# A graph-attention kernel on one core: one quad's rows loaded singly by SyncE, and a new order at the end

## Chip, core, metric

The kernel runs on one core of a Trainium2 chip. The metric is the device time of one execution in microseconds (us); of several runs the median is given.

## The reference

200,000 edges lead from `src` to `dst` among 12,500 nodes; `dst` is sorted. The node features are normalised, and a graph attention layer with four heads of 32 values is added to the input:

```
h = relu(layernorm(x));  hn = h @ W_node.T;  e = edge_attr @ W_edge.T
att = leaky_relu(sum([hn[src], hn[dst], e] * a), 0.2)          # one value per edge and head
m = max(segment_max(att, dst), 0);  ex = exp(att - m[dst])
denom = segment_sum(ex, dst) + (E - deg) * exp(-m)
out = x + segment_sum(ex / denom[dst] * hn[src], dst)
```

## The kernel before

Edges are cut into 392 groups of 511 (512 places, the first one for what is carried over from the group before); a group is four chunks of 128 edges (`J = 4`), and four groups are a quad (`QG = 4`). There are 98 quads, counted from 0. First a stage turns all nodes into rows of a table in HBM, `table`, with 137 numbers (548 bytes) a row. Then each quad goes through these steps:

- **Gather.** `gather` (L171 on) lets POOL (GpSimd) issue one indirect DMA per chunk: 128 rows of `table`, one for each partition, picked by `srci`. They land in `ga_all`, which has eight places of one quad each (`QUADS = 8`, place `q % 8`). Sixteen such DMAs are one quad. They are asked for two quads ahead of the logits (`fetch(q + 2)` in `open_logits`) and run when the place is free; a semaphore of the place, `arrived`, counts them. For quad 97 the last, half empty group has two fewer.
- **Logits.** `all_logits` (L1395 on) multiplies edge features `ea` and marks `at` (L658, made by DVE from the targets `db`) on PE, L688 and L691. `ea` is loaded by SyncE (SP) two quads ahead, `db` one quad ahead. From quad 10 on `db` holds bytes and fills a quarter of each of the two places in `db_all`, a tile of 16 KB a partition.
- **Sources.** `add_sources` (L720 on) has ScalarE (ACT) wait for the quad's gathers and copy their source terms to `U` (L735).
- **Softmax.** `softmax(s)` (L771 on) works on two to four quads at once (a "super"): scans on DVE, an exponential on ACT (L877), transposes on PE.
- **Sums.** `sums(q)` (L1061 on) weighs the gathered rows (L1048, L1089), marks targets (`hot`, L1031, L1091) and multiplies on PE (L1122), window by window: `for i in range(m)` goes over the four groups. When a quad's sums are done, its place in `ga_all` is free.
- **Division.** `divide_ranges` (L1315 on) for quads below 75, `divide` (L1360 on) after that, turn sums into results; SyncE stores them.

SyncE has one queue in program order. Loads and stores are put on lists (`due`) and issued by `issue` (L598) at fixed points of these steps. Some take their address from SBUF: `windows` (L584) reads register values, one per window, with `values_load_multi_w_load_instructions`. Quads 0 to 35 have one window, 36 to 74 two, later ones four.

The last quads go through `finale` (L1552 on), where the order of the generators `older` (sums of quads 95 and 96), `turned_stage` and `turned_last` (the last two softmaxes), and the divisions is written out by hand. There POOL weighs some rows too (L1048 on POOL), and one division runs on POOL (`divide_by_gpsimd`). `copied_out` (L995 on) makes `den`, the exponential that a division starts from; the first step of a division is L1371. `const_ps` is one PSUM bank for constants and small operands, such as `share_ps`.

Of the kernel before, what the change touches and what calls it, by code (L numbers as in the profile page):

```python
# [9 lines left out]
F32 = mybir.dt.float32  # L10
BF16 = mybir.dt.bfloat16
I32 = mybir.dt.int32
U8 = mybir.dt.uint8
AF = mybir.ActivationFunctionType
OP = mybir.AluOpType
AX = mybir.AxisListType

P = 128
H, HD = 4, 32
# [9 lines left out]
J = 4  # L29
GE = J * P  # L30
NE = GE - 1
WIDE, NARROW = 112, 80
QG = 4
# [6 lines left out]
QUADS = 8  # L40
# [6 lines left out]
SQUARE = 32  # L47
TWO = 2
HELD = 3
SETS = max(NODE_T, QG * J)  # L50
PAD = 1 << 20

# [17 lines left out]
def kernel(  # L70
# [95 lines left out]
    ga_all = consts.tile([P, QUADS, QG, J, ROW], F32, name="ga")  # L166
    GA, GATHERED = {}, set()
    arrived = [tc.alloc_semaphore(f"rows{k}") for k in range(QUADS)]
    landings = {}

    def gather(q, rows, width, lo, hi):  # L171

        g0, m = quads[q]
        ga = GA[q] = ga_all[:, q % QUADS]
        chunks = lambda i: -(-min(E - (g0 + i) * NE + 1, GE) // P)
        for i in range(lo, hi):
            if chunks(i) < J:
                nc.vector.memset(ga[:, i, chunks(i):, :], 0.0)
        order = [(i, j) for i in range(lo, hi) for j in range(chunks(i))]
        for i, j in order:  # L180
            came = nc.gpsimd.indirect_dma_start(  # L181
                out=ga[:, i, j, 0:width], out_offset=None, in_=rows,
                in_offset=bass.IndirectOffsetOnAxis(ap=srci[:, g0 + i, j:j + 1], axis=0))
            if q >= QUADS:
                came.then_inc(arrived[q % len(arrived)], 16)
                tc.no_tile_sem_insts.add(came.ins.name)
                tc.add_to_no_dep_group(f"rows{q}", came.ins)
                landings[q] = landings.get(q, 0) + 16
# [27 lines left out]
    with tc.manual_schedule():  # L216
# [165 lines left out]
        def fetch_targets(q):  # L382
            g0, m = quads[q]
            n = P if class_of(q)[1] == WIDE else NARROW
            db, rows = db_all[:, q % 2], dst.rearrange("(g e) -> g e", e=GE)
            if q >= OFFSETS:
                db = db.rearrange("p g e -> p (g e)")[:, 0:QG * GE // 4].bitcast(U8)
                db, rows = db.rearrange("p (g e) -> p g e", e=GE), offset
            DB[q] = db
            return [(db[:n, lo:lo + k, :],  # L390
                     rows[g0 + lo:g0 + lo + k].unsqueeze(0).to_broadcast([n, k, GE]))
                    for lo, k in blocks(m, QG if q >= OFFSETS else PLACES_BY)]
# [150 lines left out]
    with tc.tile_pool(name="work", bufs=2) as work, \  # L543
# [13 lines left out]
        kept = WIDE + W + QG * H + 1  # L557
        assert kept + GE // per + 1 <= 512
        kept_ps = const_ps[:, kept:kept + GE // per + 1]
        nc.vector.tensor_copy(lane_ps, lane)  # L560
        nc.vector.tensor_copy(node_ps, node_at)
        nc.vector.tensor_copy(part_ps, part)
# [72 lines left out]
        def fetch_rows(s):  # L635
            g0, m = groups(s)
            dr = DR[s] = turned.tile([SBG * H, NE + 2], I32, name="dr", bufs=2)
            if finer(s) > 1:
# [4 lines left out]
            nc.sync.dma_start(dr[0:H * m, :],  # L643
                              dst_rows[g0:g0 + m, :].unsqueeze(0).to_broadcast([H, m, NE + 2]))

        def open_logits(q):
            if q == supers[of_quad[q]][0]:
                fetch_rows(of_quad[q])
            if q + 2 < nq:
                fetch(q + 2)  # L650
            AT[q] = work.tile([P, QG, GE], BF16, name="at")
# [68 lines left out]
        def add_sources(q):  # L720

            s = of_quad[q]
            g0, m = quads[q]
            s0, sm = groups(s)
            keep_logits(q)
            if s not in U:
                U[s] = turned.tile([P, J, SBG * H], F32, name="U", bufs=2)
            f = finer(s)
            u = U[s][:, 0:J // f, 0:sm * H * f].rearrange("p c (h w) -> p w c h", h=H)[
                :, (g0 - s0) * f:(g0 - s0 + m) * f]  # L730
            if q >= QUADS:
                nc.scalar.wait_ge(arrived[q % len(arrived)],
                                  sum(landings[a] for a in range(QUADS, q + 1)
                                      if a % len(arrived) == q % len(arrived)))
            taken = nc.scalar.copy(u, GA[q][:, :m].rearrange("p g (f c) r -> p (g f) c r", f=f)[  # L735
                :, :, :, R_SRC:R_SRC + H])
            if q >= QUADS:
                tc.declare_no_dep(taken.ins, group=f"rows{q}",
                                  reason="a semaphore counts the gathers of this quad")
                tc.declare_fence(taken.ins, group=f"rows{q}")  # L740
            for kept in (EA, DB, PW, AT):
                del kept[q]
# [10 lines left out]
        def keeps(s):  # L753

            f = finer(s)
            R = groups(s)[1] * H * f
            n = (NE if f == 1 else GE // f) + 1
            dr = DR.pop(s)
            earlier = dr[:R, 0:n]
            if 0 < s < len(supers) - 1:  # L760
                before_ps = ps.tile([P, GE], F32, name="t_ps")
                nc.scalar.copy(before_ps[:R, 0:n], earlier)
                earlier = before_ps[:R, 0:n]
            elif s:
                nc.scalar.copy(kept_ps[:R, 0:n], earlier)
                earlier = kept_ps[:R, 0:n]
            kp = KP[s] = turned.tile([SBG * H, GE + 1], F32, name="kp")
            nc.vector.tensor_tensor(kp[:R, 1:n + 1], dr[:R, 1:n + 1], earlier,
                                    op=OP.is_equal)
# [134 lines left out]
        def complete(window=True, all_due=False):  # L904

            state["step"] += 1
            division = None
            if divisions and "hold" not in state and (
                    all_due or divisions[0][-1] is None or divisions[0][-1] + 2 <= state["step"]):
                division = divisions.pop(0)  # L910
            if begun and window:
                complete_window(*begun.pop())
            if division:
                divide(*division)
# [74 lines left out]
        def due_division():  # L989

            if not divisions:
                copied_out()
            return divisions.pop(0)

        def copied_out():  # L995

            if "to copy" not in state:
                return
            q, i, pt, acc = state.pop("to copy")
            span = class_of(q)[1]  # L1000
            nc.scalar.copy(pt[:1 + span, i, :], acc)

            parts = (2,) if first_fold - 2 <= q < first_fold else ()
            if i + 1 in parts or i == windows_in[q][1] - 1:
                lo = max([at for at in parts if at <= i], default=0)
                den = work.tile([P, QG, H], F32, name="den", bufs=4)
                nc.scalar.activation(den[:1 + span, lo:i + 1, :],
                                     pt[:1 + span, lo:i + 1, R_SRC:R_SRC + H], AF.Exp, scale=-1.0)
                divisions.append((q, pt, den, lo, i + 1, None))
# [51 lines left out]
        def sums(q):  # L1061
# [36 lines left out]
            for i in range(m):  # L1098
# [31 lines left out]
                if not later and i == (2 if k > 1 else 1):  # L1130
                    entered()
                    if k == 1:
                        settled()
                complete(new)
                if k == 1:
                    begun.append((q, i, ga, hot, pt, acc, fc))
                if i == 2 and QUADS <= q < first_fold - 5 and of_quad[q + 1] == s:
# [414 lines left out]
        def finale(s, held_sums):  # L1552

            def step(*of):
                for one in of:
                    next(one, None)

            state["hold"] = True
            turned_stage, last = softmax(s), nq - 1
            last_hot, last_lg = marked(last), last_logits(last)  # L1560
            older = chain(sums(last - 2), sums(last - 1))
            step(turned_stage, last_lg, last_lg, turned_stage)
            together(held_sums)
            step(last_lg, last_lg, turned_stage)
            complete()
            copied_out()
            step(turned_stage, turned_stage)
            together(turned_stage)
            select(s + 1)
            turned_last = softmax(s + 1)  # L1570
            step(older)
            added = divide(*due_division(), whole=False)
            keeps(s + 1)
            step(older)
            added()
            together(check_steps)
            step(older)
            together(last_hot)
            step(older)
            divide(*due_division(), whole=False)()  # L1580
            step(turned_last, turned_last, turned_last, turned_last)
            beside_rows(last - 1)
            RESTED.add(last - 1)
            step(older, turned_last, older, older, turned_last, older)
            divide_by_gpsimd(*due_division())
            together(turned_last)
            topped()
            redo = nc.values_load(flag[0:1, 0:1], min_val=0, max_val=1)
            together(older)
            return redo  # L1590
# [282 lines left out]
```

## Time and profile before

| what | value |
|---|---|
| median of 3 runs | 1997.35 us (1996.39 to 2000.05) |
| profiled execution | 1993.67 us |
| its span from first to last instruction | 1991.8 us |
| busy: POOL, DVE, PE, ACT | 75%, 60%, 57%, 16% of the span |
| mean granted TensorE clock | 0.734 |
| table gathers on POOL | 1494, 946 ns each |

An engine's busy share leaves out register, semaphore and DMA-issuing instructions, so SyncE has none there; what it issues and what it waits for has views of its own, in which it is named SPq. A wait is put down to what ended it. "issue" means that nothing in the profile was waited for.

### The profile page before, as it was taken

To read this page: it belongs to the slowest core of one execution; us is meant where nothing else is said; L and a number is where in the kernel's file an instruction comes from. 1 tells how busy PE (TensorE), PEld (TensorE's weight loads), DVE (VectorE), ACT (ScalarE), POOL (GpSimd) and SP (SyncE) were. 2 spreads that over 40 slices of the span, in tenths; PEclk is the share of its full clock that TensorE was granted. 3 is DMA by queue.
4 is the path that set the end of the run, shared out by engine and by line. 5 is a ranking of instruction groups with operands and counts; after the bars stand their busy time and mean duration, and the time that the engine had idled before them with its cause. 6 is when DMAs were issued, how large, how long until landed. Compare 5 with 4: busy or idle time off the path is not lost. (4 is left out here: it accounts for less than half of the span.)

```text
span 1991.8 us, 18871 instructions
## 1 busy us (share of the span) xinstructions
PE 1140.5 (57%) x5116; PEld 780.2 (39%) x5116; DVE 1193.3 (60%) x2615; ACT 318.3 (16%) x1077; POOL 1491.3 (75%) x1585
## 2 busy tenths in 40 slices
PE   6566676556464655554646555546465555455565
PEld 5444454334243433342434333334343333233344
DVE  8676786456374554564746546647465474367676
ACT  6564111001011010010110100101000011122122
POOL 7777777777777777777777777777777777777774
PEclk9788788676676776767767767677777666777778
DMA  7754754434344444344444444444444444444442
GB/s 254 209 141 98 175 132 111 105 93 110 97 108 104 119 98 114 96 108 112 119 101 113 106 110 108 108 114 115 104 107 105 105 120 98 112 109 116 99 106 51
DMA packets 167748, 229.57 MB, mean 115 GB/s; under 512 B 60827, under 2 KB 100669, under 8 KB 167638
## 3 DMA queue, kind: packets, MB, share of 16 engines
q0 software_dynamic: 50112, 109.61, 24.7%
q1 hardware_dynamic: 115824, 116.14, 20.5%
q10 hardware_dynamic: 1702, 2.59, 0.4%
q8 instruction: 41, 0.67, 0.1%
q14 instruction: 69, 0.57, 0.1%
HBM read 210.74 MB, written 17.43 MB: 115 GB/s over the span
## 5 line engine op out<-in xcount | busy, mean ns | idle before, releaser
L181 POOL DMA_INDIRECT ga<-table,srci x1494 | 1413.7, 946 | 456.0 <-issue 407.9
L1122 PE MATMUL acc<-ga,hot 128*113 128x137 f32 (+1 forms) x2928 | 546.2, 346 | 81.5 <-DVE hot L1031 53.6
L1122 PEld LDWEIGHTS acc<-ga,hot 128*113 128x113 f32 (+1 forms) x2928 | 486.5, 216 | 182.2 <-issue 100.4
L956 DVE SCALAR_TENSOR_TENSOR pt<-pt,spare,acc 1x133 f32<-1x133 f32 x113 | 38.3, 339 | 523.5 <-ACT den_of L950 522.1
L691 PE MATMUL lg<-at,pw 112*96 112x512 bf16 (+2 forms) x392 | 157.2, 438 | 278.7 <-DVE at L658 265.8
L688 PE MATMUL lg<-ea,by_pair 128*96 128x512 f32 (+1 forms) x392 | 229.6, 671 | 7.1 <-ACT tg L701 7.1
L658 DVE TENSOR_TENSOR at<-const_ps,db 112x1024 bf16<-112x1024 f32 (+1 forms) x176 | 212.8, 1210 | 3.3 <-DMA db<-offset 3.3
L1089 DVE TENSOR_TENSOR ga<-ga,ex_ps 128x1056 f32<-128x1056 f32 x147 | 182.2, 1239 | 0.0
L792 PE MATMUL t_ps<-ident,U 128*64 128x128 f32 (+2 forms) x210 | 47.2, 397 | 208.9 <-ACT U L735 208.9
L735 ACT COPY U<-ga 128x64 f32<-128x64 f32 x98 | 29.0, 297 | 806.5 <-DMA ga<-table,srci 806.5
L1091 DVE TENSOR_TENSOR hot<-const_ps,slot 128x896 f32<-128x896 f32 (+1 forms) x147 | 144.1, 980 | 0.0
L792 PEld LDWEIGHTS t_ps<-ident,U 128*64 128x64 f32 (+2 forms) x210 | 37.1, 201 | 234.9 <-ACT U L735 231.6
L887 PE MATMUL ex_ps<-ident,stack 128*128 128x128 f32 x105 | 28.6, 424 | 170.2 <-DVE stack L879 157.0
L975 PEld LDWEIGHTS acc<-pt,spare 1*2 1x2 f32 x226 | 14.1, 86 | 209.0 <-issue 200.8
L691 PEld LDWEIGHTS <-pw 112*96 112x96 bf16 (+2 forms) x392 | 54.4, 139 | 102.2 <-issue 99.1
L887 PEld LDWEIGHTS ex_ps<-ident,stack 128*128 128x128 f32 x105 | 18.5, 215 | 184.3 <-ACT stack L877 184.3
L1048 DVE TENSOR_TENSOR ga<-ga,ex_ps 128x528 f32<-128x528 f32 x92 | 63.6, 693 | 38.6 <-ACT xs L893 38.5
L181 POOL DMA_INDIRECT ga<-in_x_dram,srci x72 | 68.3, 948 | 23.2 <-issue 19.2
L701 ACT COPY tg<-lg 96x512 f32<-96x512 f32 (+1 forms) x51 | 29.5, 578 | 293.8 <-PE lg L691 284.4
L920 PE MATMUL acc<-ga,hot 128*81 128x137 f32 x176 | 43.2, 334 | 52.7 <-ACT ga L928 50.8
L717 PE MATMUL t_ps<-tg,of_head 96*64 96x512 f32 (+3 forms) x96 | 72.5, 848 | 0.0
L717 PEld LDWEIGHTS t_ps<-tg,of_head 96*64 96x64 f32 (+3 forms) x96 | 12.0, 174 | 154.1 <-issue 150.9
(209 smaller groups left out, 1318.6 us busy)
## 6 DMA issues: line engine op xcount, KB each, us to landing
ea<-in_edge_t_dram SPq DMA_DIRECT2D x196, 256.0 KB
ga<-table,srci POOLq DMA_INDIRECT x1494
db<-offset SPq DMA_DIRECT2D x53, 256.0 KB
db<-in_dst_dram SPq DMA_DIRECT2D x20, 320.0 KB
db<-offset SPq DMA_DIRECT2D x35, 160.0 KB
table<-row SPq DMA_DIRECT2D x9, 616.5 KB
xt<-in_x_dram SPq DMA_DIRECT2D x9, 576.0 KB
inputs<-in_x_dram SPq DMA_DIRECT2D x92, 56.0 KB
```

The source lines that it names most:

```text
L181: came = nc.gpsimd.indirect_dma_start(out=ga[:, i, j, 0:width], out_offset=None, in_=rows, in_offset=bass.IndirectOffsetOnAxis(ap=srci[:, ...
L658: nc.vector.tensor_tensor(AT[q][:span, i:i + n, :].rearrange("p g e -> p (g e)"), part_ps[:span].to_broadcast([span, n * GE]), DB[q][:span ...
L688: nc.tensor.matmul(lg, by_pair[:, begin:begin + n], ea[:, i // 2, :], start=half == 0 and i == 0, stop=False, skip_group_check=True)
L691: nc.tensor.matmul(lg, PW[q][:span, begin:begin + n], at[:span, i, :], start=False, stop=full and i == quads[q][1] - 1, skip_group_check=True)
L717: nc.tensor.matmul(TP[s][:groups(s)[1] * H], of_head[supers[s][1], p][:n], tg[:n], start=p == 0, stop=False, skip_group_check=True)
L792: nc.tensor.matmul(t_ps[:R, j * P:(j + 1) * P], u[:, j, :R], ident, start=False, stop=j == C - 1, skip_group_check=True)
L887: nc.tensor.transpose(turned_ps[:, j, :], stack[:, j * P:(j + 1) * P], ident)
L920: nc.tensor.matmul(acc, hot[:, i, 0, 0:acc.shape[0]], ga[:, i, 0, :], start=False, stop=stop)
L1048: engine.tensor_tensor(val, val, weight.unsqueeze(3).to_broadcast([P, J, H, HW]), op=OP.mult)
L1089: nc.vector.tensor_tensor(val, val, weight.unsqueeze(3).to_broadcast([P, TWO * J, H, HW]), op=OP.mult)
L1091: nc.vector.tensor_tensor(hot[:, i:i + TWO, :, 1:1 + span].rearrange("p g j c -> p (g j) c"), lane_ps[:, 0:span].unsqueeze(1).to_broadcast ...
L1122: nc.tensor.matmul(acc, hot[:, i, j, 0:1 + span], ga[:, i, j, :], start=new and j == J - 1 and not second, stop=k > 1 and i % k == k - 1 a ...
```

## The change

Quad 84 (the 85th) is no longer gathered by POOL. Its 2048 rows are loaded by SyncE, one DMA a row, into a part of `db_all` that is free from quad 10 on; for that, the two places of `db` lie next to each other at its start. The loads are spread over the sums of quads 11 to 74: after each window, `single_rows` issues eight of them; every second time it first reads sixteen addresses into registers. The addresses of a chunk (128 source numbers) are loaded into one partition sixteen windows ahead (`fetch_places`) and scaled to bytes by DVE (`scale_places`). ScalarE waits for two semaphores, each counting half of the rows, before it copies the quad's source terms.

At the end, `den` of quad 95's first division lies in PSUM, and the steps of `finale` have another order.

```diff
+SINGLE, SINGLES_FROM, AT_A_STEP = 84, 11, 8
...
     def gather(q, rows, width, lo, hi):
+        if q == SINGLE:
+            return
...
             if q >= OFFSETS:
-                db = db.rearrange("p g e -> p (g e)")[:, 0:QG * GE // 4].bitcast(U8)
+                at = q % 2 * QG * GE // 4
+                db = db_all.rearrange("p k g e -> p (k g e)")[:, at:at + QG * GE // 4].bitcast(U8)
...
+        GA[SINGLE] = own[:, QG * GE // 2:QG * GE // 2 + n_own].bitcast(F32).rearrange(
+            "p (g j r) -> p g j r", g=QG, j=J)
...
+        def fetch_places(n):
+            if n >= QG * J:
+                return
+            g, j = quads[SINGLE][0] + n // J, n % J
+            at = ((g // 2 * J + j) * 2 + g % 2) * P
+            nc.sync.dma_start(places[n % 2], src[at:at + P].unsqueeze(0))
+        def scale_places(n):
+            if n < QG * J:
+                nc.vector.tensor_scalar(places[n % 2], places[n % 2], float(4 * ROW), None,
+                                        op0=OP.mult)
+        def single_rows():
+            if not single["step"]:
+                fetch_places(0)
+                scale_places(0)
+            n, at = divmod(single["step"], steps)
+            if n >= QG * J:
+                return
+            single["step"] += 1
+            if not at:
+                fetch_places(n + 1)
+            if at == steps // 2:
+                scale_places(n + 1)
+            lo = at * AT_A_STEP
+            if at % 2 == 0:
+                single["values"] = nc.values_load_multi_w_load_instructions(
+                    places[n % 2][:, lo:lo + 2 * AT_A_STEP], engines=[mybir.EngineType.SP], ...)[1]
+            for p in range(lo, lo + AT_A_STEP):
+                came = nc.sync.dma_start(
+                    as_bytes(GA[SINGLE][p:p + 1, n // J, n % J, :]),
+                    rows_at(table, single["values"][p - at // 2 * 2 * AT_A_STEP], 4 * ROW, 1))
+                came.then_inc(single_came[2 * n // (QG * J)], 16)
...
             if q == SINGLE:
+                for came in single_came:
+                    nc.scalar.wait_ge(came, single["landings"] // 2)
...
-                den = work.tile([P, QG, H], F32, name="den", bufs=4)
+                den = den_ps if q == first_fold - 2 and not lo else work.tile(
+                    [P, QG, H], F32, name="den", bufs=4)
...
                 complete(new)
+                if q >= SINGLES_FROM:
+                    single_rows()
...
             turned_last = softmax(s + 1)
-            step(older)
-            added = divide(*due_division(), whole=False)
-            keeps(s + 1)
-            step(older)
-            added()
+            step(older, older)
+            divide(*due_division(), whole=False)()
             together(check_steps)
             step(older)
+            keeps(s + 1)
             together(last_hot)
             step(older)
             divide(*due_division(), whole=False)()
-            step(turned_last, turned_last, turned_last, turned_last)
             beside_rows(last - 1)
             RESTED.add(last - 1)
-            step(older, turned_last, older, older, turned_last, older)
+            step(turned_last, turned_last, older, turned_last, turned_last, older)
+            step(turned_last, older, older, turned_last)
             divide_by_gpsimd(*due_division())
```

More of the change, by code (lines that the diff above doesn't have):

```diff
@@ L168 @@
     arrived = [tc.alloc_semaphore(f"rows{k}") for k in range(QUADS)]
+    single_came = [tc.alloc_semaphore(f"single{k}") for k in range(2)]
     landings = {}
     def gather(q, rows, width, lo, hi):
+        if q == SINGLE:
+            return
         g0, m = quads[q]
@@ L559 @@
         kept_ps = const_ps[:, kept:kept + GE // per + 1]
+        den_at = kept + GE // per + 1
+        assert den_at + QG * H <= 512
+        den_ps = const_ps[:, den_at:den_at + QG * H].rearrange("p (g h) -> p g h", h=H)
         nc.vector.tensor_copy(lane_ps, lane)
@@ L644, in fetch_rows @@
                               dst_rows[g0:g0 + m, :].unsqueeze(0).to_broadcast([H, m, NE + 2]))
+        own = db_all.rearrange("p k g e -> p (k g e)")
+        n_own = QG * J * ROW
+        GA[SINGLE] = own[:, QG * GE // 2:QG * GE // 2 + n_own].bitcast(F32).rearrange(
+            "p (g j r) -> p g j r", g=QG, j=J)
+        places = [own[0:1, QG * GE // 2 + n_own + k * P:QG * GE // 2 + n_own + (k + 1) * P]
+                  for k in range(2)]
+        single = {"step": 0, "landings": 0}
+        steps = -(-P // AT_A_STEP)
+        def fetch_places(n):
[23 more added lines that the diff above has]
+                single["values"] = nc.values_load_multi_w_load_instructions(
+                    places[n % 2][:, lo:lo + 2 * AT_A_STEP], engines=[mybir.EngineType.SP],
+                    min_val=0, max_val=(NP - 1) * 4 * ROW,
+                    skip_runtime_bounds_check_because="a node's row")[1]
+            for p in range(lo, lo + AT_A_STEP):
[3 more added lines that the diff above has]
+                came.then_inc(single_came[2 * n // (QG * J)], 16)
+                tc.no_tile_sem_insts.add(came.ins.name)
+                tc.add_to_no_dep_group(f"rows{SINGLE}", came.ins)
+                single["landings"] += 16
         def open_logits(q):
@@ L730, in add_sources @@
                 :, (g0 - s0) * f:(g0 - s0 + m) * f]
-            if q >= QUADS:
+            if q == SINGLE:
+                assert single["landings"] == 16 * P * QG * J
+                for came in single_came:
+                    nc.scalar.wait_ge(came, single["landings"] // 2)
+            elif q >= QUADS:
                 nc.scalar.wait_ge(arrived[q % len(arrived)],
-                                  sum(landings[a] for a in range(QUADS, q + 1)
-                                      if a % len(arrived) == q % len(arrived)))
+                                  sum(landings[a] for a in range(QUADS, q + 1) if a != SINGLE
+                                      and a % len(arrived) == q % len(arrived)))
             taken = nc.scalar.copy(u, GA[q][:, :m].rearrange("p g (f c) r -> p (g f) c r", f=f)[
```

## The prediction

> **What bounds the kernel now.** I read the page first, then the POOL rows in order of time, then who waited for whom, then SyncE's own queue.
>
> ```profile
> span 1991.8 us, 18871 instructions
> PE 1140.5 (57%) x5116; PEld 780.2 (39%) x5116; DVE 1193.3 (60%) x2615; ACT 318.3 (16%) x1077; POOL 1491.3 (75%) x1585
> ...
> L181 POOL DMA_INDIRECT ga<-table,srci x1494 | 1413.7, 946 | 456.0 <-issue 407.9
> ...
> L735 ACT COPY U<-ga 128x64 f32<-128x64 f32 x98 | 29.0, 297 | 806.5 <-DMA ga<-table,srci 806.5
> ```
>
> The busiest engine is POOL at 75%, but the rest of its time is mostly the issue of the same gathers: 408 of the 456 us ahead of them wait for nothing. The consumer of the gathered rows, the copy to U, waited 806 us for them. In order of time (columns: start, duration, what; in brackets the idle time before):
>
> ```profile
> 1041.00 0.94 POOL L181 DMA_INDIRECT ga<-table,srci  x1 [0.30 <-issue]
> 1042.25 0.94 POOL L181 DMA_INDIRECT ga<-table,srci  x1 [0.30 <-issue]
> 1043.50 0.94 POOL L181 DMA_INDIRECT ga<-table,srci  x1 [0.30 <-ACT xs L893]
> ...
> 1183.36 0.95 POOL L181 DMA_INDIRECT ga<-table,srci  x1 [0.30 <-issue]
> ```
>
> One gather every 1.25 us without a hole: 16 of them, 20.0 us, are one quad, and POOL sets the pace. The gather at 1042.25 is the last of quad 51 (counted from 0). Its U copy follows 1.7 us after the gather's end at 1043.19, and the last matmul of its sums ends at 1134.71:
>
> ```profile
> 1044.85 0.31 ACT L735 COPY U<-ga 128x64 f32<-128x64 f32 x1 [1.00 <-DMA ga<-table,srci]
> ...
> 1133.46 1.25 PE L1122 MATMUL acc<-ga,hot 128*113 128x137 f32 x8
> ```
>
> There are eight places for gathered quads. Quad 59 takes over quad 51's place at 1183.36, 48.7 us after it came free. So everything behind POOL may run 49 us later than now before POOL itself has to wait: that is the ring's slack.
>
> **SyncE, where the change puts the work.** The stretch in which the single loads run is that of the sums of quads 11 to 74, 64 quads of 32 records each:
>
> ```profile
> L1122 PE MATMUL acc<-ga,hot x2048: 277/281/575, 325.3 to 1593.2; 128*113 128x137 f32 x155, 128*81 128x137 f32 x32
> ```
>
> SyncE's waits in that stretch (total us, times, longest):
>
> ```profile
> SPq L598 <- DVE res L1333: 841.0, 64, 17.2
> SPq L598 <- PE lg L691: 71.5, 34, 4.7
> SPq L598 <- DMA out_dram<-res: 26.4, 36, 1.6
> SPq L598 <- PE acc L1122: 4.7, 14, 0.9
> ```
>
> Together 944 us of 1268 are waits (the rows below these are under 3 us each). So 944 us are free, 14.7 us of each 20 us quad; the rest is work that stays.
>
> **The change part by part.**
>
> Single loads: 16 chunks of 128 rows are 2048 DMAs of 548 bytes, eight after each window of the sums, 32 a quad. Each row costs SyncE three things: its address read into a register, a register move, the issue. The trace has all three kinds, though not in these sizes. Register loads (ns, least/median/most), with one, two and four values in an instruction as the classes of quads have one, two and four windows:
>
> ```profile
> L584 SPq TENSOR_LOAD <-base_row x19: 264/270/291, 331.8 to 688.1; - x19
> ...
> L584 SPq TENSOR_LOAD <-base_row x32: 470/476/576, 872.7 to 1489.4; - x32
> ...
> L584 SPq TENSOR_LOAD <-base_row x16: 863/884/1009, 1616.0 to 1893.9; - x16
> ```
>
> 0.27, 0.48, 0.88 us: 0.2 us a value. Sixteen values then take 0.27 + 15 x 0.204 = 3.3 us, with the gap behind it 0.21 us a row. Issue: the nearest rows for one piece in one partition are two small loads on ScalarE's queue; SyncE's own go to 64 or more.
>
> ```profile
> L1493 ACTq DMA_DIRECT2D rows<-in_dst_ends_dram x1: 245/245/245, 425.8 to 425.8; - x1
> L1170 ACTq DMA_DIRECT2D rows<-in_fine_ends_dram x1: 266/266/266, 1795.5 to 1795.5; - x1
> ...
> L598 SPq DMA_DIRECT2D ea<-in_edge_t_dram x127: 357/422/1346, 331.3 to 1590.2; - x127
> ...
> L598 SPq MOVE inputs<-in_x_dram x105: 29/29/37, 332.1 to 1590.7; - x105
> L598 SPq DMA_DIRECT2D inputs<-in_x_dram x105: 317/322/569, 332.2 to 1590.8; - x105
> L598 SPq DMA_DIRECT2D out_dram<-res x101: 334/345/361, 330.9 to 1591.3; - x101
> ```
>
> The two small ones average 0.255 us. They stand alone; a DMA of SyncE that does not follow a wait (inputs, 322) is 7% shorter than one that does (out, 345), so I take 0.24 us. Lower bound: no row shows an issue below 0.245, and I keep 0.21. Upper bound: 0.322, SyncE's own with an address from a register. Between the end of one DMA and the start of the next one with such an address:
>
> ```profile
> 1030.07 0.35 SPq L598 DMA_DIRECT2D out_dram<-res  x1
> 1030.47 0.42 SPq L598 DMA_DIRECT2D ea<-in_edge_t_dram  x1
> ...
> 1035.07 0.38 SPq L598 DMA_DIRECT2D db<-offset  x1
> 1035.56 0.36 SPq L598 DMA_DIRECT2D pw<-side  x1
> ```
>
> 1035.56 - 1035.45 = 0.11 us, the 29 ns move in it (without a move it is 0.05). A row thus takes 0.21 + 0.11 + 0.24 = 0.56 us, and the whole 2048 x 0.56 = 1147 us, with 5 us for the 16 loads of places: 1152 us. There are 944 free. **SyncE is short by 208 us** and becomes the pace of quads 11 to 74: 32 x 0.56 = 17.9 us in place of 14.7 free ones a quad.
>
> What of it reaches the end. SyncE's queue is in order, and behind each eight single loads stand the stores of results and the loads of ea, db, pw, dr and inputs; DVE L658 (db), PE L688 (ea) and DVE L1333 (inputs, result buffers) wait for them. The tightest is db, loaded one quad ahead: issued at 1035.07 to 1035.45, used here
>
> ```profile
> 1055.39 1.21 DVE L658 TENSOR_TENSOR at<-const_ps,db 112x1024 bf16<-112x1024 f32 x1
> ```
>
> 19.9 us later; less 1.7 us to land (the gather above), SyncE may fall 18 us behind at no cost. Then the sums fall behind, which the ring's 49 us cover. After that POOL waits for a free place: 208 - 18 - 49 = 141 us.
>
> The 16 gathers of quad 84 leave POOL: -20.0 us, whole, because POOL is the pace again after quad 74 and nothing else of its queue changes. Whether PE and DVE use the lead that POOL then has:
>
> ```profile
> 1593.00:1963.00 370.00, 207.44 (x905) 141.16 (x904) 236.90 (x488) 69.58 (x295) 280.66 (x295) 0.73 0.44 107
> ```
>
> DVE's 236.9 us must fit into some 15 x 20 + 13 = 313 us, 76%. I take 0; if the chain of waits doesn't allow it, up to the ring's 49 us come back on top.
>
> ScalarE's wait for the two semaphores at quad 84 comes ten quads after the last single load: 0. The 16 scalings of 128 numbers lie on DVE, 60% busy: 0. The new place of db follows memory that is no longer read: 0.
>
> End of the kernel. DVE's first division step of quad 95 takes 2.74 us, its like later 0.14, and it ends just when POOL's five multiplications do (1967.99):
>
> ```profile
> 1965.94 0.27 ACT L797 ACTIVATE low<-t_ps 64x128 f32<-64x128 f32 x1 [0.52 <-PE t_ps L792]
> ...
> 1965.27 2.74 DVE L1371 SCALAR_TENSOR_TENSOR den<-pt,den 81x8 f32<-81x8 f32 x1 [1.24 <-ACT den L1007]
> ...
> 1969.29 0.28 DVE L800 TENSOR_TENSOR t_ps<-t_ps,low 64x128 f32<-64x128 f32 x1
> ...
> 1979.22 0.14 DVE L1371 SCALAR_TENSOR_TENSOR den<-pt,den 81x8 f32<-81x8 f32 x1
> ...
> 1962.71 5.28 POOL L1048 TENSOR_TENSOR ga<-ga,xe 128x528 f32<-128x528 f32 x5
> ```
>
> With den in PSUM I take 0.14; the four steps behind it are unchanged, L800 has its input at 1966.21 and comes at 1966.8 in place of 1969.29: -2.5 us (0 if the operand's place is not the reason). [...] The moved older groups shift a few copies of 0.2 to 0.3 us: 0, within 1 us.
>
> Sum: +141 - 20 - 2.5 = +118.5 us. The profiled execution took 1993.67 us, so 2112; the median of the runs shown is 3.7 us above that, so 2116.
>
> **The rivals.**
>
> Hidden, faster. If a row costs 0.49 us or less, 2048 x 0.49 + 5 = 1009 us fit into 944 + 18 + 49 = 1011, POOL never waits, and only the -22.5 is left: 1971 against the profiled execution, 1975 against the median. It is decided at (1011 + 22.5 - 5) / 2048 = 0.502 us a row for no change. For it: the sixteen values come by one instruction, which no row shows beyond four, and a cheaper load of many values would do it alone; idle SyncE, 944 us, is large. Against it: 0.2 us a value is straight through three sizes.
>
> Dearer issue. If the single DMAs take 0.322 us like SyncE's others, a row is 0.64 us: 1311 + 5 - 1011 = 305, less 22.5, 2276, and up to 49 more. If they take 0.422 us like ea, it is 0.74 us and 1516 + 5 - 1011 - 22.5 = 487 more, 2481. [...] The 245 and 322 ns rows speak against it.
>
> No gain though hidden: if the quads behind 84 are held by PE's and DVE's chains, the 20 us come back as waits there: 1997. Against it stand the 806 us of U's waits.
>
> **How the numbers follow.** Forecast 0.68, with a range of its own of 2060 to 2250 (issue 0.21 to 0.31 us). Dearer 0.07, 0.03 of it at 0.422. Hidden and faster 0.20. No gain 0.03, and 0.02 for a small loss below 2060. Within 0.2% (4 us, about what a measurement of this kernel tells from no change) lies 0.03, so slower 0.77. The range reaches from the hidden case, 1970, to 2250, and leaves out the dearer issue.
>
> **What would show it.** SyncE's wait for DVE res L1333 all but gone between 325 us and the end of quad 74; register loads near 3.3 us, single DMAs near 0.24; POOL no longer one gather per 1.25 us in that stretch but waiting for PE, and U hardly waiting; afterwards POOL at its pace again, 16 gathers fewer in all; L1371 in the end at 0.14 us. Wrong, if register loads of sixteen values or DMAs of one row are much cheaper than these rows: then SyncE still waits for DVE in every quad, and the end comes 20 us sooner.

## The result and the profile after

The changed kernel takes 1972.98 us (median of 4 runs, 1972.07 to 1975.48), the kernel before 1997.61 (4 runs, 1996.39 to 2000.05). The ratio is 0.988 [0.9868, 0.9893]: 24.6 us faster, where 2116 us were forecast. The prediction was wrong in the sign; what came is its rival "hidden, faster", which it put at 1975 us.

The profiled execution took 1973.07 us, 20.6 less than the profiled execution before. The rows of the page after that answer to those shown of before:

```profile
span 1971.2 us, 23138 instructions
PE 1134.6 (58%) x5116; PEld 771.6 (39%) x5116; DVE 1193.8 (61%) x2631; ACT 318.1 (16%) x1077; POOL 1477.5 (75%) x1569
...
L185 POOL DMA_INDIRECT ga<-table,srci x1478 | 1399.8, 947 | 451.8 <-issue 408.9
...
L798 ACT COPY U<-ga 128x64 f32<-128x64 f32 x97 | 28.7, 297 | 786.7 <-DMA ga<-table,srci 786.7
```

There are 16 gathers fewer, and U still waits 787 us for gathers: POOL still sets the pace. PE's and DVE's work is the same within 6 us. POOL's own waits, in the whole span (total us, times, longest):

```profile
POOL ga L185 <- issue: 427.8, 1403, 0.3
POOL ga L185 <- PE acc L1186: 6.7, 22, 0.3
```

No wait of it is longer than 0.3 us in these rows: it never stood still for a free place. SyncE, whose lack of time was to be the new bound, still waits in the stretch of the single loads (325 to 1593 us):

```profile
SPq L606 <- DVE res L1399: 40.2, 24, 4.2
SPq L606 <- DMA rows<-in_dst_rows_dram: 26.5, 4, 8.5
SPq L692 <- DVE db L674: 12.9, 1, 12.9
SPq L606 <- DMA rows<-in_dst_ends_dram: 8.3, 1, 8.3
```

With the smaller rows, not shown, 112 us, in place of 944. Some 11 of them lie before the stretch: the wait of 12.9 us, for the first scaled addresses, begins at 313.6 us. So about 840 us of its free time were used, and 100 were left. The price of one row is in SyncE's instructions (ns least/median/most, first and last start in us):

```profile
L692 SPq TENSOR_LOAD <-db x128: 971/1167/1210, 326.5 to 1593.6; - x128
...
L697 SPq MOVE db<-table x2048: 29/29/38, 327.7 to 1601.6; - x187
L697 SPq DMA_DIRECT2D db<-table x2048: 224/228/469, 327.8 to 1601.7; - x187
```

A load of sixteen values takes 1.10 us in the mean (1.153 with the gap behind it), which is 0.07 us a row; 3.3 us and 0.21 us a row had been taken. Move, gaps and issue together take 0.337 us a row in the mean. 2048 x 0.337 + 128 x 1.153 = 838 us.

The end of the kernel after:

```profile
1943.96 0.95 POOL L185 DMA_INDIRECT ga<-table,srci  x1 [0.30 <-issue]
...
1944.92 5.29 POOL L1112 TENSOR_TENSOR ga<-ga,xe 128x528 f32<-128x528 f32 x5
...
1947.19 0.17 DVE L1437 SCALAR_TENSOR_TENSOR const_ps<-pt,const_ps 81x8 f32<-81x8 f32 x1 [0.30 <-ACT const_ps L1071]
```

The last gather ends at 1944.9, 17.8 us sooner than before (1962.7, where POOL's five multiplications began). Behind it the kernel takes 26.3 us, 2.8 less than before.

### The profile page after: what moved, and what is told of

It is laid out like the page before. It is cut to its first block, busy times and chain, and to the rows that moved or that the text cites. A ratio compares the mean times of both kernels' runs of the same rounds, so it can differ in the third digit from the quotient of the medians.

```text
span 1971.2 us, 23138 instructions
## 1 busy us (share of the span) xinstructions
PE 1134.6 (58%) x5116; PEld 771.6 (39%) x5116; DVE 1193.8 (61%) x2631; ACT 318.1 (16%) x1077; POOL 1477.5 (75%) x1569
## 4 chain that ended last, share of the span: by engine, by line
POOL 29%; DVE 27%; PE 15%; issue 13%; DMA 9%; ACT 5%; SPq 2%; ACTq 0%; POOLq 0%; DVEq 0%
POOL ga L185 29%; DMA ga<-table,srci 6%; PE acc L1186 6%; DVE at L717 4%; PE t_ps L855 2%; PE lg L747 2%; DVE ga L1112 2%; DVE t_ps L869 1%; DVE t_ps L868 1%; DVE t_ps L935 1%; DVE t_ps L932 1%; PE lg L750 1%; DVE pt L1019 1%; DVE hot L1095 1%; PE ex_ps L950 1%
## 5 line engine op out<-in xcount | busy, mean ns | idle before, releaser
L1186 PE MATMUL acc<-ga,hot 128*113 128x137 f32 (+1 forms) x2904 | 536.3, 344 | 83.9 <-DVE hot L1095 43.4
L1186 PEld LDWEIGHTS acc<-ga,hot 128*113 128x113 f32 (+1 forms) x2904 | 476.5, 214 | 183.8 <-issue 78.9
L185 POOL DMA_INDIRECT ga<-in_x_dram,srci x72 | 68.5, 951 | 23.3 <-issue 18.9
L747 PEld LDWEIGHTS lg<-ea,by_pair 128*96 128x96 f32 (+1 forms) x392 | 63.4, 187 | 13.2 <-ACT tg L760 8.6
```

The costliest lines, as they stand in the source:

```text
L185: came = nc.gpsimd.indirect_dma_start(out=ga[:, i, j, 0:width], out_offset=None, in_=rows, in_offset=bass.IndirectOffsetOnAxis(ap=srci[:, ...
L747: nc.tensor.matmul(lg, by_pair[:, begin:begin + n], ea[:, i // 2, :], start=half == 0 and i == 0, stop=False, skip_group_check=True)
L1186: nc.tensor.matmul(acc, hot[:, i, j, 0:1 + span], ga[:, i, j, :], start=new and j == J - 1 and not second, stop=k > 1 and i % k == k - 1 a ...
```

## The experiments

The theory: the time of this change is set by whether SyncE's work for the rows fits into its free time; the forecast failed because sixteen values in a row, at a good place, load much faster (1.10 us) than the rows of one, two and four values had suggested (3.3). Rivals: that single DMAs also hide otherwise (SyncE's lag doesn't reach POOL, so the load's price doesn't matter), or that the gain comes from the end's new order.

The first eight kernels, e1 to e8, ran on two chips on which many of SyncE's instructions took about 0.7 us each (in e1 410 of 2325 took 0.68 to 0.72 us, in the profile before one) and the kernel before took 2404 and 2403 us. So from these eight only the durations of instructions are used, and those kernels that matter were run again on other chips, where the kernel before took 1994 to 1995 us. Ratios are to the kernel before on the same chip.

**The end alone (e1, f3), and `den` in PSUM alone (e3), on the kernel before.**

```diff
+        den_ps = const_ps[:, den_at:den_at + QG * H].rearrange("p (g h) -> p g h", h=H)
...
+                den = den_ps if q == first_fold - 2 and not lo else work.tile(
+                    [P, QG, H], F32, name="den", bufs=4)
...          (e1 and f3 also: the new order of steps in finale)
```

> The kernel before with the change of its end alone: den of quad 95's first division in PSUM, and the new order of the last steps. All rows still come through POOL. Theory (the end is worth what the stalled division step was): 2.5 to 3 us less than before, 1994.5 to 1995; in the trace L1371's 2.74 us is about 0.17. Rival (the end's part is larger, and the single loads give less than 20 us): 4 to 8 us less, 1990 to 1993. Rival (nothing): within 0.5 us of before.

> The kernel before with den of quad 95's first division in PSUM alone, the old order of the last steps kept. Theory (the division step waits for POOL's multiplications only because both of its operands lie in SBUF): the whole gain of the end, 2.5 us, stands here, 1995; the step takes 0.17 us although POOL's five multiplications run beside it. Rival (the step waits for something else, and the new order is what helped): no change, and the step again takes 2.7 us.

> The kernel of e1 once more, on a chip where SyncE runs evenly: the new end alone. Theory: 2.5 to 3 us less than before. Rivals: nothing, within 0.5 us; or 4 to 8 us less.

Measured: e1 2401.0, ratio 0.9998 [0.9976, 1.0019]; e3 2402.39, 0.9999 [0.9983, 1.0015]: both inconclusive, as their intervals are wider than the effect. f3: 1992.08 against 1994.87, 0.9986 [0.9977, 0.9996], -2.8 us. Its end:

```profile
1963.38 5.29 POOL L1052 TENSOR_TENSOR ga<-ga,xe 128x528 f32<-128x528 f32 x5
...
1967.33 0.17 DVE L1375 SCALAR_TENSOR_TENSOR const_ps<-pt,const_ps 81x8 f32<-81x8 f32 x1 [0.30 <-ACT const_ps L1011]
```

The division step takes 0.17 us inside POOL's multiplications, where it had taken 2.74. The end alone is worth 2.8 us of the 24.6, by its interval 0.8 to 4.6. In e3's trace the step comes 3.5 us after POOL's multiplications and so doesn't test its place. But in e1 and e3 other division steps, with both operands in SBUF, did run beside them: they took 0.38 to 0.61 and 1.03 us, where the same steps take 0.17 and 0.18 when POOL isn't multiplying (both in e3).

**The single loads alone, with the old end (e2, f2).**

```diff
-                den = den_ps if q == first_fold - 2 and not lo else work.tile(
-                    [P, QG, H], F32, name="den", bufs=4)
+                den = work.tile([P, QG, H], F32, name="den", bufs=4)
...          (and the old order of steps in finale)
```

> The changed kernel with the old end: single loads of quad 84, but den in SBUF and the old order of the last steps. Theory: POOL's chain is 16 gathers of 1.25 us shorter and nothing else changes, 20 us less than before, 1977 to 1978; L1371's first step (its line has moved) takes 2.7 us again. Rival (the single loads give more than their gathers): 1973 or less. Rival (part is lost again behind quad 84): 1980 or more.

> The kernel of e2 once more, on a chip where SyncE runs evenly: single loads of quad 84 with the old end. Theory: POOL's chain is 16 gathers of 1.25 us shorter and SyncE's 0.40 us a row are hidden: 20 us less than before. Rival (part of it is lost behind quad 84, where two quads' work must fit into one quad's gathers): 10 to 17 us less. Rival (more than the gathers): 24 us less.

Measured: e2 2633.86, 1.0943 [1.0901, 1.0986], on one of the two chips where SyncE itself was slow. f2: 1975.98, 0.9906 [0.989, 0.9923], -18.9 us. In f2 the division step is long again:

```profile
1943.90 2.67 DVE L1436 SCALAR_TENSOR_TENSOR den<-pt,den 81x8 f32<-81x8 f32 x1 [1.03 <-ACT den L1070]
...
1941.27 5.28 POOL L1111 TENSOR_TENSOR ga<-ga,xe 128x528 f32<-128x528 f32 x5
```

-18.9 and -2.8 make -21.7 in sum; a second run of the whole change on a chip of this kind (g4, below) gives -23.4, and the difference lies within the intervals. So the singles bring nearly all of it.

**The load's price: one value an instruction (e5, f5), four (e6, f4), sixteen shifted by one word (e7, g1).**

```diff
-                single["values"] = nc.values_load_multi_w_load_instructions(
-                    places[n % 2][:, lo:lo + 2 * AT_A_STEP], ...)[1]
+                single["values"] = []
+                for k in range(0, 2 * AT_A_STEP, 1):             # e5, f5; by 4 in e6, f4
+                    single["values"] += nc.values_load_multi_w_load_instructions(
+                        places[n % 2][:, lo + k:lo + k + 1], ...)[1]
```

```diff
-        places = [own[0:1, QG * GE // 2 + n_own + k * P:QG * GE // 2 + n_own + (k + 1) * P]
+        places = [own[0:1, QG * GE // 2 + n_own + 1 + k * P:QG * GE // 2 + n_own + 1 + (k + 1) * P]
```

The second diff is e7 and g1: the same sixteen values, one word further on.

> The changed kernel with the sixteen addresses read by sixteen register loads of one value each in place of one load of sixteen. SyncE alone has more work; the queue model of the prediction is put to the test with sizes that the rows now show. Issue with move and gaps takes 0.32 us a row, a load of one value 0.27 + 0.05: 0.64 us a row, 1311 + 5 us against 944 free, 18 of lead and 49 of slack in the ring. Theory (SyncE's own time decides, and the prediction failed by the size of the loads alone): POOL waits for free places for about 305 us, the time is about 1973 + 305 = 2278, 2200 to 2350. Rival (SyncE's queue doesn't hold up the others as the model says): under 2050.

> The changed kernel with four register loads of four values each. Theory A (a load costs 0.2 us for each value, and only long loads are cheaper): 0.88 us each as in the rows of base_row with four values, 0.55 us a row, 1130 us against 1011: about 1973 + 120 = 2090. Theory B (a load costs 0.2 us for each aligned piece of 16 bytes, and the loads of base_row lie across such pieces): 0.27 to 0.3 us each, 0.40 us a row, hidden: 1973. The duration of the loads in the trace tells them apart at once.

> The changed kernel with the addresses one word (4 bytes) further on in SBUF, so that no load of sixteen starts at a multiple of 16 bytes. Theory B (aligned pieces of 16 bytes): the loads take 5 pieces or fall back to single values, 1.2 to 3.3 us in place of 0.97 to 1.19; with 3.3 us a row is 0.53 us and the time 2050 or more. Theory A (the number of values decides, not where they lie): the loads stay at 0.97 to 1.2 us and the time at 1973.

> The kernel of e5 once more, on a chip where SyncE runs evenly: sixteen register loads of one value, 0.27 us each, so 0.32 + 0.27 + 0.05 = 0.64 us a row, 1316 us in all against 944 free, 18 of lead and 49 of slack. Theory (the prediction's model of SyncE's queue holds, only its register loads were mis-sized): POOL waits some 305 us, the time is 280 to 290 us above before (230 to 340). Rival (SyncE's lateness isn't passed on, or only after a larger lead): less than 60 us above before.

> The kernel of e6 once more: four register loads of four values. Its loads took 0.30 us each in e6, so a row takes 0.32 + (0.30 + 0.05) / 4 = 0.41 us, 840 us in all against 1011. Theory (SyncE's time decides, and aligned pieces of 16 bytes make the loads cheap): hidden, the time of the changed kernel, about 20 to 24 us under before. Rival (0.2 us for each value): 95 us above before.

> The kernel of e7 once more, on a chip where SyncE runs evenly: the changed kernel with its addresses one word further on in SBUF, so that a load of sixteen takes 3.46 us (e7), 0.22 us a row. That is the price which the prediction took, 0.21. Theory (the load's price was the one wrong term of the sum): the time that was forecast, 2116, or with the rows' measured 0.337 us for move and issue 128 x 3.51 + 2048 x 0.337 = 1139 us against 944 + 18 + 49: 128 us of waiting, 2101; up to 2150 if the ring's slack isn't won back. Rival (another term was wrong as well): under 2050 or over 2200.

The load's rows of f5, f4 and g1, in this order:

```profile
L694 SPq TENSOR_LOAD <-db x2048: 260/268/511, 324.6 to 2029.1; - x187
```

```profile
L694 SPq TENSOR_LOAD <-db x512: 292/298/642, 324.7 to 1599.6; - x171
```

```profile
L692 SPq TENSOR_LOAD <-db x128: 3268/3464/3536, 326.4 to 1808.7; - x128
```

By the medians one value takes 0.27 us, four neighbours 0.30, sixteen 1.17; the same sixteen shifted by a word 3.46. The runs e5, e6 and e7 gave medians of 0.268, 0.296 and 3.459 for these (their times: 2972.87, 2658.21 and 2869.34 us; 1.2356, 1.1048, 1.1926). So among the shifted sixteen a value costs about 0.2 us (3.46 / 16), and four neighbours that start at a multiple of four words, counted from the start of their tile, cost little more than one. Whether a smaller multiple would do was not tried. It is not every piece of four words that counts once, as theory B has it: two neighbours of `base_row`, which begin at even words of their tile, took 0.48 us.

The times: f4 1972.19, 0.989 [0.9873, 0.9906], no different from the changed kernel, as its loads, 512 x 0.33 us in the mean or 169 us, still fit into the free time like the 128 x 1.10 = 141 there. f5 2349.63, 1.1781 [1.1761, 1.18]: 355 us above the kernel before, more than the 230 to 340 expected. g1 2131.42, 1.0686 [1.0668, 1.0704]: 136 above. g1 is the decisive one: with nearly the price that the prediction took for sixteen values (3.46 us for 3.3), everything else as in the changed kernel, the time is 2131 us where 2116 had been forecast. POOL's waits in f5 and in g1:

```profile
POOL ga L185 <- issue: 422.5, 1386, 0.3
POOL ga L185 <- PE acc L1188: 335.7, 83, 8.9
POOL ga L185 <- ACT t_ps L827: 37.4, 5, 7.7
POOL ga L185 <- PE acc L985: 29.0, 6, 27.5
```

```profile
POOL ga L185 <- issue: 420.5, 1379, 0.3
POOL ga L185 <- PE acc L1186: 153.9, 60, 7.7
POOL ga L185 <- PE acc L983: 25.3, 6, 23.8
```

The row PE acc L1186, 6.7 us in the changed kernel, is 153.9 in g1: POOL now stands still for sums that come late, the way that the prediction told. Between 325 and 1593 us U now waits 125 us for gathers, before 677. And SyncE no longer waits for DVE; of the 841 us before, in f5 these are left:

```profile
SPq L606 <- DVE res L1401: 2.8, 12, 0.4
```

The rival that SyncE's lag would stay hidden in any case has fallen.

**Twice as many at a step (e8, g2).** The same loads in half the stretch: sixteen rows after each window.

```diff
-SINGLE, SINGLES_FROM, AT_A_STEP = 84, 11, 8
+SINGLE, SINGLES_FROM, AT_A_STEP = 84, 11, 16      # and a load of sixteen at each step
```

> The changed kernel with sixteen single loads after each window in place of eight, so that they are done with quad 42 in place of 74. Same total work, twice as dense: 64 rows x 0.39 us = 25 us in each quad's 20, of which 14.7 are free. Theory (SyncE's time per quad decides): 32 quads x 10.3 us = 330 us short, less 67 of lead and slack, so about 260 us later than the changed kernel, 2235 (2180 to 2290), although nothing is added. Rival (later quads make it good again, since SyncE is freer there): under 2050.

> The kernel of e8 once more: sixteen single loads after each window in place of eight, done with quad 42 in place of 74; same work in all, and sixteen-value loads as in the changed kernel. Theory (SyncE's time in each quad decides, not its total): quads 11 to 42 need 838 us of SyncE where about 480 are free, 290 us of waiting after lead and slack, 2265 (2220 to 2330). Rival (later quads make it good again): under 2050.

Measured: e8 2850.76 (1.1849); g2 2247.21, 1.127 [1.1251, 1.1289], 252 above the kernel before. Loads cost the same as in the changed kernel; only the free time that they have is less:

```profile
L692 SPq TENSOR_LOAD <-db x128: 971/1159/1201, 325.0 to 1306.5; - x128
...
POOL ga L185 <- PE acc L1186: 265.3, 49, 12.3
```

It is the free time per quad that decides, as the theory had it (2220 to 2330). The same work that is hidden at 32 rows a quad costs 252 us at 64. Behind 1320 us POOL's row PE acc L1186 grows by only 2.1 us, but what was lost by then isn't made good.

**Another quad: `SINGLE = 96` (e4, f1).** Whether a later quad leaves POOL as well.

```diff
-SINGLE, SINGLES_FROM, AT_A_STEP = 84, 11, 8
+SINGLE, SINGLES_FROM, AT_A_STEP = 96, 11, 8
```

> The changed kernel with quad 96 loaded singly in place of quad 84 (one number changed). Theory (POOL sets the pace up to its last gather, and which quad it leaves out doesn't matter to that): POOL ends at the same time, and the time is that of the changed kernel, 1973, within 2 us. Rival (with quad 96's rows long there, the softmax of quads 95 and 96 comes 20 us sooner and the tail behind the last gather has less to do): 2 to 6 us less, 1967 to 1971. Rival (the order written out by hand for the end is upset): 2 us or more above 1973.

> The kernel of e4 once more, since in the runs e1 to e8 SyncE itself ran in fits, many of its instructions taking 0.7 us each, and the kernel before took 2404 us there. Where SyncE runs evenly: theory (POOL sets the pace, whichever quad it leaves out) 1973, within 2 us; rival (the tail behind the last gather gets shorter) 1967 to 1971; rival (the order of the end is upset) 1975 or more.

Measured: e4 2627.12 (1.0927). f1 1989.16 against 1994.41, 0.9973 [0.9963, 0.9983]: only 5.2 us gained, so the theory's 1973 is missed, and the rival came by which the end is upset. The end of f1:

```profile
1940.33 0.94 POOL L185 DMA_INDIRECT ga<-table,srci  x1 [0.30 <-issue]
...
1954.29 1.09 POOL L1112 TENSOR_TENSOR ga<-ga,xe 128x528 f32<-128x528 f32 x1 [13.02 <-ACT xe L953]
```

POOL's last gather ends at 1941.3, even sooner than in the changed kernel, but the kernel ends at 1985.2, 43.9 us later in place of 26.3: POOL's own multiplications wait 13.0 us for ScalarE, and then 7.0 us more, as the softmax of the last quads isn't done. The likely reason: in the last quads a quad whose rows come free of charge leaves the other engines only one quad's gathers' time for the logits, softmax and sums of two; quad 84 lies where 13 quads' time follow to make up for it. That these waits come from this and not from another delay of that softmax wasn't tried apart.

**Five groups: also the first group of quad 85 (g3), in the hope of more.**

```diff
+        if q == SINGLE + 1:
+            lo = 1                                     # in gather: group 0 of quad 85 left out
...
+        CHUNKS = QG * J + J                            # the last four into one_more
...
+                nc.scalar.wait_ge(single_came[2], 16 * P * J)
+                moved = nc.scalar.copy(GA[q][:, 0], one_more)
...
+                    if i == 1 and q % 3:
+                        single_rows()
```

> A version meant to beat both: besides quad 84, the first group of quad 85 (512 rows more) is loaded singly, into the last free part of db_all, and ScalarE copies it to its place in the ring before it copies quad 85's source terms. A second set of eight rows is added after the second window of two quads in three, so that the loads end with quad 79. POOL does 4 gathers fewer. Theory (SyncE's need, 512 x 0.41 = 210 us more, just fits into the 106 us left, 67 of lead and slack and what quads 75 to 79 leave): 5 us under the changed kernel, 1968. Rival (SyncE is short by some tens of us and POOL waits): 10 to 60 us above the changed kernel.

> The changed kernel itself, beside the three others on the same chip, so that they are compared with it and not with its earlier runs. Expected by every theory: 22 to 25 us under before.

g4 is the changed kernel unaltered, beside it: 1971.65 against 1995.02, 0.9883 [0.9867, 0.99]. g3 took 2014.89, 1.0099 [1.0082, 1.0116], slower than both: 43 us above the changed kernel, where its rival had 10 to 60. Of POOL's waits:

```profile
POOL ga L187 <- PE acc L997: 52.3, 7, 21.9
```

51.7 us of it lie between 1600 and 1800 us. Four more chunks at 1.25 us would have saved 5 us of POOL; but behind the rows' 838 us SyncE had some 100 us to spare, and a quarter more is some 210. Of its waits between 325 and 1593 us 19 us are left, without the wait for the first addresses. This version fails for the reason for which the changed kernel had been expected to fail.

## Why the prediction was wrong

**The step that failed** is one term: "Sixteen values then take 0.27 + 15 x 0.204 = 3.3 us, with the gap behind it 0.21 us a row". It measured 1.10 us, 1.153 with the gap, 0.07 us a row. The three rows it came from (0.27, 0.48 and 0.88 us) are right, but all three are values of one array, `base_row`, and the prediction took the number of values for the only thing that sets the price. g1 shows that their place sets it as much: 3.46 us for the same sixteen, shifted by one word. Why `base_row`'s four take 0.88 and four of f4 only 0.30 is likely the same: by the program its values for quad 75 start at word 114 of the tile (36 quads with one value, 39 with two), and all later fours like these two words past a multiple of four. But `base_row` wasn't moved, so for it this is argued, not shown.

**The other terms of a row** held: 0.234 us in the mean (median 0.228) for the issue where 0.24 was taken, and 0.337 with move and gaps where 0.35 was. The rival "dearer issue" had no part in it: the 0.322 and 0.422 us of its two cases were not reached, neither by the mean nor by the median.

**The sum** was 2048 x 0.56 + 5 = 1152 us; with the right load it is 838, against 944 free. The point from which the prediction let it turn, 0.502 us a row, lies between what was measured on its two sides: 0.41 a row (838 / 2048) is faster by 24.6 us, 0.43 (f4) by 22.7, 0.55 (g1) slower by 136. One term was left out, as the rest of SyncE's time was taken as "work that stays": the 128 register loads of `base_row` and `base_side` for quads 11 to 74, which were there before, became longer by 23 us in all (last section). With these and the 4 us for the loads of places the changed kernel's SyncE has 865 us more to do, some nine of them behind 1593 us; that agrees within 2% with the 840 us of free time that were used.

**The queue and the ring** behaved as told where SyncE is short. From the means of the traces, g1's work is 691 us of moves and issues, 442 of its loads, 23 of longer loads and 4 for the places: 1160, short by 216; less 18 and 49, less 22.5, this makes 2122 on the 1995 of that chip; measured 2131. For f5 the same way 692 + 659 + 23 + 4 = 1378, 1995 + 434 - 67 - 22.5 = 2340; measured 2350. Both are some 10 us longer than this sum, as if 57 us were covered in place of 67. The 18 were read at a single quad; whether they are smaller elsewhere, or SyncE loses the time otherwise, is open. That g1's 2131 lies so near the forecast 2116 is in part luck: moves and issues had been taken 26 us too dear, and the longer loads and the smaller cover, 33 us, were not in the sum.

**The 16 gathers** were taken as -20.0; f2 measured -18.9, and the last gather ends 17.8 us sooner (in g4's trace 20.7). **`den` in PSUM** was taken as -2.5 and the moved groups as 0; f3 measured -2.8, and the step went from 2.74 to 0.17. That the operand's place is the reason, on which the -2.5 rests, was the author's assumption; no run shows it by itself. What the runs showed: with both operands in SBUF the step took 2.74 us before and 2.67 in f2, and ended within 0.03 us of POOL's multiplications both times; with `den` in PSUM it took 0.17 beside them in f3, where the order of steps was new as well. What each of the two parts of the end brings by itself was not measured: e3's time tells nothing, and f3 has both.

**The rival that came** had been given 0.20, and its condition was named: a cheaper load of many values "would do it alone". Against it the prediction set that "0.2 us a value is straight through three sizes". Three sizes of one array at one kind of place don't bear an extrapolation to four times the largest, when the sign hangs on a threshold 10% below the sum (0.502 against 0.56 us a row).

## What to carry to other kernels

An engine's idle queue can take work from the engine that sets the pace (f2: -18.9 us), if that queue's own instructions are counted, row by row, against its free time in that stretch; here the limit lies between 0.43 and 0.55 us a row. Where a forecast hangs on a threshold, ask which of its prices has been measured in another form only (another place, another count), and give the other side a chance to match. Values that go into registers should lie together and, as far as these runs show, start at a multiple of four words: four took 0.30 us (f4) where one took 0.27 (f5), and sixteen shifted by one word 3.46 (g1) where they had taken 1.17.

## What the runs showed of the hardware

Reading values from SBUF into registers: one 0.27 us (f5), four that start at a multiple of four words 0.30 (f4), sixteen that do 0.97 to 1.2 (the changed kernel), sixteen shifted by one word 3.46 (g1).

The register loads that were there before became longer when single DMAs stand ahead of them. After:

```profile
L592 SPq TENSOR_LOAD <-base_row x19: 443/539/690, 343.3 to 699.8; - x19
...
L592 SPq TENSOR_LOAD <-base_row x32: 663/688/825, 878.2 to 1499.4; - x32
...
L592 SPq TENSOR_LOAD <-base_row x17: 864/880/973, 1627.3 to 1897.4; - x17
```

Those with one and two values, 0.27 and 0.48 us before, take 0.54 and 0.69; those with four, which come after the last single load, are unchanged at 0.88. The loads of `base_side` behave alike (0.47 and 0.67 us), and its seven loads of four that still fall between the single loads take 1.07 us, in place of 0.87. In g2 the single loads end at 1313 us, and the loads of two values are short again behind them:

```profile
L592 SPq TENSOR_LOAD <-base_row x14: 530/672/797, 871.1 to 1280.8; - x14
...
L592 SPq TENSOR_LOAD <-base_row x15: 469/473/498, 1329.8 to 1546.0; - x15
```

So it is the single DMAs between them that go with the longer loads; by what way they do it was not tried.

On two chips SyncE was slow in fits, while the gathers on POOL kept their duration (944 ns in the mean in e1, 946 before); there the kernel before took 2404 and 2403 us, and the single loads made it slower by 9% (e2). A change that fills a queue's last free time is worth something only as long as that queue keeps its pace.
